# State sum by accumulating transfers, y times gate on GpSimd, d and du repeated inside SBUF, conv norm's moments on ScalarE, with new order tables

## The chip, the cores and the metric

The kernel runs on one core of a Trainium2 chip. The metric is the device time of one execution in microseconds (us); the median of several executions is given. PE is TensorE (matrix products into PSUM), DVE VectorE, ACT ScalarE, POOL GpSimd, and SP SyncE, which only starts transfers. POOL reads and writes SBUF alone, not PSUM. Each engine takes its instructions strictly in order, so an instruction that waits holds up all that stands behind it on its engine.

## The reference, cut to what matters

The input x is (4, 64, 64, 96): four images of L = 4096 tokens with C = 96 channels. Layer 0 normalizes (group norm, then a layer norm over the channels, called c norm here), projects each token to value u, gate, delta d and three blocks A, B, C of 96 x 16 states, and runs a recurrence along the tokens:

```
proj = layernorm(groupnorm(x)) @ W_in + b_in
value, delta = proj[..., :C], proj[..., 2*C:3*C];  gate = sigmoid(proj[..., C:2*C])
h_new = d * (A_t * h) + d * (B_t * u)          # per channel and state, S = 16
y = gate * sum over states of (C_t * h_new)
x = x + y @ W_out + b_out
```

Layer 1 adds a linear attention (no softmax, six heads, so that it comes down to one matrix per image made from the Gram matrix of the normalized tokens) and a feed-forward block in fp8 with fp16 rounding, each behind a layer norm (a norm and f norm).

## The kernel before, in words

An image is cut into NCH = 8 chunks of TC = 512 tokens; the N = 32 chunks of all images, called groups g here, run one after the other, since the recurrence goes along them. A group is NT = 12 tiles: four blocks sh of four states each, times three blocks cg of 32 channels. A tile is 128 partitions (4 states x 32 channels) by 512 tokens. There are K = 384 tiles, and the main loop makes one step per tile (the loop over s at the end of the kernel). In step s it issues, in this order: the B projection of tile s+3 (three matmuls into the one bank B) and its copy to SBUF with bias on ACT (`b_copy`, L888), the A projection of tile s+1, the C projection of tile s, ACT's copy of the last state, on POOL the multiply of B by du for tile s+2 (`b_mul`, L891) and, where the tile is one of the list ON_POOL, the multiply of C by h of tile s-1 (`c_mul_pool`, L940), on DVE the scan of tile s (L907), the A multiply by d of tile s+1 (`a_mul`, L900) and, for tiles not on ON_POOL, the C multiply (`c_mul`, L931, reads PSUM). For a tile on ON_POOL, ACT first copies C from PSUM to SBUF (`c_copy`, L937). Then everything that the table AT puts at this step is issued (`call(step)`).

AT is an order written out by hand: it names for each piece of work a step relative to the first step s0 of its group. Negative steps prepare a group ahead, steps of 12 and more finish it beside the next group's tiles, and the FFN of a group runs 96 steps later (beside the next image), at its own offsets. Work that would fall behind step K goes to a planner (`Plan`), which orders the end by costs, ranks and a random search; another such plan orders the start.

What the change touches, with its lines:

- d and du: `d_out` (ACT, L786) and `du_out` (DVE, L790) leave d and d*u of a group in `dd`, 96 partitions by 2 x 512. The tiles need them repeated for each of the four states of a partition block: `write` (L824) sends `dd` to DRAM, and `read` (L831) reads it back four times, once per block of 32 partitions, into `rep` (two buffers). SP starts both.
- the state sum: the products of C and h lie in one buffer of 3 x 512 per block sh (`slot`, L925): block 0 in the ring "cha" of two, blocks 1, 2, 3 in the ring "chb" of three. `gather` (L946) adds each of blocks 1, 2, 3 into block 0's buffer by an accumulating transfer started on POOL, at steps 7, 11 and 14. `state_sum` (L955, step 18) sums the four states on the partitions and turns them to channels with three matmuls against the matrix `fold` into PSUM; an fp32 matmul shows as two instructions. `gated` (DVE, L993, step 18) multiplies that by the gate.
- the norms: `LayerNorm.stats` makes mean and variance on DVE (four BATCH_NORM_STATS2, L433, and four BATCH_NORM_AGGREGATE, L435). `Roots.root` on POOL adds eps (L406), raises to the power -1/2 (L409), negates the mean (L412) and multiplies it (L413). `apply` on ACT (L450) scales and shifts, with two pointer operands.
- x tiles wait in XBUFS = 15 buffers from `load_x` to `total`, where the output is formed.

## Time and profile before

Three runs of the kernel took 1170.11 us in the median (1169.56 to 1172.9). The profiled execution:

| what | value |
|---|---|
| time of the profiled execution | 1169.27 us |
| its span, first to last instruction | 1167.5 us |
| mean granted clock of TensorE | 0.992 |
| first scan of the first group; first scan of the last group; end of the last scan | 35.1; 1073.1; 1104.0 us |
| groups of image 0 and 1 (35.1 to 303.0) | 32 to 36 us each |
| groups 17 to 25 (600.2 to 871.4) | 33.4 to 34.7 us each |
| the end (1104.0 to 1167.5): busy DVE, ACT, POOL | 48.5, 44.2, 24.8 us of 63.5 |
| accumulating gathers (768 KB), start to landing, median | 6.6 us |
| read of rep (384 KB each of four); write of dd | 7.3; 3.2 us |
| DVE's waits, all: on the out projection (L1003) | 17.2 us in 29 times |
| B's weight loads waiting for ACT | 22.5 us in 33 times |

The page's groups give a line of the code, engine, operation, tiles written and read, shapes and count, then busy time and mean duration, then the idle time ahead of them. In the timeline each row has start, duration, engine, line and operation; rows marked x4 are four instructions merged. A busy share says how full an engine is, but instructions of one engine overlap at their ends, and TensorE's ends are modelled, so the distance between starts is the better price of an instruction on a full engine.

### The profile page before, as it was taken

To read this page: it belongs to the slowest core of one execution; us is meant where nothing else is said; L and a number is where in the kernel's file an instruction comes from. 1 tells how busy PE (TensorE), PEld (TensorE's weight loads), DVE (VectorE), ACT (ScalarE), POOL (GpSimd) and SP (SyncE) were. 2 spreads that over 40 slices of the span, in tenths; PEclk is the share of its full clock that TensorE was granted. 3 is DMA by queue.
4 is the path that set the end of the run, shared out by engine and by line. 5 is a ranking of instruction groups with operands and counts; after the bars stand their busy time and mean duration, and the time that the engine had idled before them with its cause. 6 is when DMAs were issued, how large, how long until landed. Compare 5 with 4: busy or idle time off the path is not lost. (4 is left out here: it accounts for less than half of the span.)

```text
span 1167.5 us, 19144 instructions
## 1 busy us (share of the span) xinstructions
PE 1129.6 (97%) x5868; PEld 865.4 (74%) x5868; DVE 1116.8 (96%) x2110; ACT 811.3 (69%) x1818; POOL 1008.9 (86%) x1166
## 2 busy tenths in 40 slices
PE   6999999999999999999999999999999999999984
PEld 5777776777777777777877777777777777777662
DVE  6999999999999999999999999999999999999986
ACT  4666656555556777777777777787777777776477
POOL 5798888888889899899999999999999999988643
PEclk7999999999999999999999999999999999999999
DMA  7577777787776777687777778667776876777321
GB/s 183 137 167 146 165 158 160 157 178 164 166 162 151 161 166 175 148 185 162 159 163 167 165 165 189 149 152 159 167 172 149 183 160 157 150 161 166 78 82 55
DMA packets 104289, 182.13 MB, mean 156 GB/s; under 512 B 42637, under 2 KB 50769, under 8 KB 104186
## 3 DMA queue, kind: packets, MB, share of 16 engines
q1 hardware_dynamic: 90060, 106.96, 38.9%
q0 software_dynamic: 13536, 73.93, 31.8%
q8 instruction: 46, 0.75, 0.3%
q14 instruction: 57, 0.47, 0.1%
q10 hardware_dynamic: 590, 0.02, 0.0%
HBM read 69.12 MB, written 24.77 MB: 80 GB/s over the span
## 5 line engine op out<-in xcount | busy, mean ns | idle before, releaser
L891 POOL TENSOR_TENSOR bu<-bu,rep 128x512 f32<-128x512 f32 x384 | 511.3, 1342 | 51.1 <-ACT state L917 39.7
L907 DVE TENSOR_TENSOR_SCAN h<-Aps,state,bu 128x512 f32<-128x512 f32 x336 | 426.1, 1268 | 0.3 <-issue 0.2
L888 ACT ACTIVATE bu<-Bps,b_bac 128x512 f32<-128x512 f32 x384 | 262.8, 684 | 198.7 <-PE Bps L283 190.8
L900 DVE SCALAR_TENSOR_TENSOR Aps<-Aps,b_bac,rep 128x512 f32<-128x512 f32 x384 | 281.8, 734 | 3.6 <-PE Aps L283 3.1
L283 PE MATMUL Bps<-xs,w 128*128 128x512 f32 x768 | 266.9, 429 | 3.4 <-ACT bu L888 3.1
L283 PE MATMUL Aps<-xs,w 128*128 128x512 f32 x768 | 241.7, 395 | 1.2 <-DVE h L907 1.0
L940 POOL TENSOR_TENSOR ch<-ch,h 128x512 f32<-128x512 f32 x126 | 168.1, 1334 | 9.7 <-ACT ch L937 5.1
L283 PEld LDWEIGHTS Aps<-xs,w 128*128 128x128 f32 x768 | 143.6, 188 | 37.2 <-DVE h L907 2.9
L283 PEld LDWEIGHTS Bps<-xs,w 128*128 128x128 f32 x768 | 126.5, 190 | 45.5 <-ACT gx_ps L632 12.6
L283 PE MATMUL Aps<-xl,w 128*128 128x512 f32 x384 | 151.8, 395 | 0.0
L283 PE MATMUL Bps<-xl,w 128*128 128x512 f32 x384 | 151.4, 394 | 0.0
L283 PE MATMUL Cps<-xs,w 128*128 128x512 f32 x384 | 120.6, 395 | 0.0
L283 PE MATMUL Dps<-xs,w 128*128 128x512 f32 x384 | 120.6, 395 | 0.0
L931 DVE SCALAR_TENSOR_TENSOR ch<-Dps,b_bac,h 128x512 f32<-128x512 f32 x160 | 118.6, 741 | 0.4
L946 POOL DMA_DIRECT2D ch<-ch x94 | 88.7, 944 | 2.3 <-DMA ch<-ch 1.7
L283 PEld LDWEIGHTS Aps<-xl,w 128*128 128x128 f32 x384 | 72.0, 188 | 17.8
L283 PEld LDWEIGHTS Bps<-xl,w 128*128 128x128 f32 x384 | 72.2, 188 | 17.5
L283 PEld LDWEIGHTS Cps<-xs,w 128*128 128x128 f32 x384 | 72.0, 188 | 17.6
L283 PEld LDWEIGHTS Dps<-xs,w 128*128 128x128 f32 x384 | 72.0, 188 | 17.6
L937 ACT ACTIVATE ch<-Cps,b_bac 128x512 f32<-128x512 f32 x94 | 64.5, 686 | 24.3 <-PE Cps L283 24.3
L283 PE MATMUL Cps<-xl,w 128*128 128x512 f32 x192 | 75.7, 395 | 0.0
L283 PE MATMUL Dps<-xl,w 128*128 128x512 f32 x192 | 75.6, 394 | 0.0
(203 smaller groups left out, 2013.7 us busy)
## 6 DMA issues: line engine op xcount, KB each, us to landing
ch<-ch POOLq DMA_DIRECT2D x94, 768.0 KB, 6.6
rep<-ddd SPq DMA_DIRECT2D x124, 384.0 KB, 7.3
ddd<-dd SPq DMA_DIRECT2D x31, 384.0 KB, 3.2
xl<-lo SPq DMA_DIRECT2D x62, 128.0 KB, 2.4
x<-in_x_dram SPq DMA_DIRECT2D x32, 192.0 KB, 3.0
xatd<-xat SPq DMA_DIRECT2D x32, 192.0 KB, 3.8
xal<-xatd SPq DMA_DIRECT2D x32, 192.0 KB, 3.4
out_dram<-o SPq DMA_DIRECT2D x32, 192.0 KB, 3.4
```

What stands on the lines that cost most here:

```text
L283: nc.tensor.matmul(ps, lhsT=wt[:, n], rhs=mv, start=(n == 0), stop=(n == 2))
L888: nc.scalar.activation(self.bu, self.b_ps, AF.Identity, bias=self.bias(0))
L891: nc.gpsimd.tensor_tensor(self.bu, self.bu, rep[self.b, self.i][:, 1, self.cg], ALU.mult)
L900: nc.vector.scalar_tensor_tensor(self.a_ps, self.a_ps, self.bias(1), rep[self.b, self.i][:, 0, self.cg], ALU.add, ALU.mult,)
L907: nc.vector.tensor_tensor_scan(self.h, self.a_ps, self.bu, 0.0 if self.i == 0 else state[self.sh, self.cg], ALU.mult, ALU.add,)
L931: nc.vector.scalar_tensor_tensor(self.slot(), self.c_ps, self.bias(2), self.h, ALU.add, ALU.mult)
L937: nc.scalar.activation(self.ch, self.c_ps, AF.Identity, bias=self.bias(2))
L940: nc.gpsimd.tensor_tensor(self.ch, self.ch, self.h, ALU.mult)
L946: nc.gpsimd.dma_start(chs[g, 0], chs.pop((g, sh)), accum_op=ALU.add)
```

## The change

- **State sum.** The buffer into which the blocks are gathered is that of block 1 (of block 0 in the very first group), it lies in ring "cha", and the others lie in "chb". After three gathers, two more accumulating transfers on POOL halve it, 128 to 64 to 32 partitions (`halve64`, `halve32`), and `collect` (three transfers on SP) puts the result on 96 partitions in a new buffer y. The three matmuls go, but for the last group, which keeps them in the plan of the end.
- **Gated** runs on POOL from y in place of DVE from PSUM; the last group stays on DVE.
- **d, du.** `spread` copies from `dd` to `rep` inside SBUF: four calls of three transfers each, and `rep` has its dimensions in another order. The write to DRAM and the reads go.
- **c norm.** In groups 2 to 31 its moments come from ACT: four activations with accumulation for the sums, one for the mean with its sign, four squares with accumulation, and one for variance plus eps. The two groups of the start stay on DVE.
- **All norms.** POOL keeps the power and the product; eps and the negated mean come from two small ACT instructions (`shifts_scalar`) in the a and f norms of the main part, from DVE in the start and the end.
- **Tables.** AT has new steps, image 0 has a table AT0 of its own, ON_POOL has three tiles per group in place of four (1, 2, 9; in image 0 0, 5, 9, of which the first group has only 9), and the end has other ranks, pairs, costs, seed and choices of engine.

The diff, cut to its core:

```diff
 AT = {
-    "load_x": -39, "centre": -25, "scale": -24, "stats": -22, "rstd": -22, "apply": -21,
-    "transpose": -14, "affine": -13, "upper": -13, "low": -12, "proj_d": -9, "d_out": -9,
-    "proj_u": -9, "du_out": -9, "write": -9, "read": -6, "proj_gate": -3, "gate_out": -1,
-    "gather1": 7, "gather2": 11, "gather3": 14,
-    "state_sum": 18, "gated": 18, "project_out": 19, "residual": 19, "stats_a": 20,
-    "rstd_a": 21, "apply_a": 22, "transpose_a": 33, "keep": 34, "spill": 39, "gram": 24,
-    "gram_out": 24, "gram_add": 26,
-    "fetch": 21, "attention": 26, "residual_f": 26, "stats_f": 26, "rstd_f": 27, "apply_f": 29,
-    "transpose_f": 30, "quant_in": 31, "hidden0": 37, "relu0": 37, "hidden1": 31, "relu1": 33,
-    "hidden2": 38, "relu2": 38, "project_f": 40, "round_out": 40, "bias_out": 40, "total": 46,
-    "store": 51,
-    "sums": -31, "sums_out": -30,
+    "load_x": -35, "centre": -28, "scale": -27, "stats": -26, "squares": -24, "rstd": -22,
+    "apply": -20, "transpose": -14, "affine": -13, "upper": -13, "low": -12, "proj_d": -9,
+    "d_out": -9, "proj_u": -8, "du_out": -8, "spread0": -7, "spread1": -5, "spread2": -5,
+    "spread3": -5, "proj_gate": 0, "gate_out": 3, "gather1": 7, "gather2": 10, "gather3": 13,
+    "halve64": 15, "halve32": 18, "collect": 21, "state_sum": 22, "gated": 24,
+    "project_out": 25, "residual": 25, "stats_a": 26, "shift_a": 26, "rstd_a": 26,
+    "apply_a": 29, "transpose_a": 35, "keep": 35, "spill": 36, "gram": 30, "gram_out": 30,
+    "gram_add": 30, "fetch": 23, "attention": 26, "residual_f": 26, "stats_f": 27,
+    "shift_f": 28, "rstd_f": 28, "apply_f": 29, "transpose_f": 30, "quant_in": 30,
+    "hidden0": 37, "relu0": 37, "hidden1": 31, "relu1": 32, "hidden2": 38, "relu2": 38,
+    "project_f": 39, "round_out": 39, "bias_out": 41, "total": 48, "store": 54, "sums": -30,
+    "sums_out": -30,
 }
 MV_BUFS = {1: 4, 2: 2}
-END_RANKS = (-2, 0, 1)
-END_PAIR = (0, 1, 1, 2, 2, 3, 3, 4)
-APPLY_DVE = (0, 2, 4, 6, 7)
-QUANT_POOL = (1, 4)
-BIAS_DVE = (0, 1, 2, 3, 4, 5, 6, 7)
-TOTAL_DVE = (1, 3, 5, 7)
-ON_POOL = (0, 2, 7, 8)
+END_RANKS = (-5, 1, -1)
+END_PAIR = (0, 1, 2, 3, 4, 5, 6, 6)
+APPLY_DVE = (1, 2, 6)
+QUANT_POOL = (0, 1, 2, 3, 5, 7)
+BIAS_DVE = (0, 3, 4, 5, 6, 7)
+TOTAL_DVE = (0, 3, 4, 5, 6)
+ON_POOL = (1, 2, 9)
+AT0 = {
+    "load_x": -35, "centre": -30, "scale": -27, "stats": -24, "rstd": -21, "apply": -17,
+    "transpose": -14, "affine": -13, "squares": -23, "upper": -13, "low": -13, "proj_d": -10,
+    "d_out": -10, "proj_u": -9, "du_out": -9, "spread0": -8, "spread1": -7, "spread2": -6,
+    "spread3": -6, "proj_gate": 0, "gate_out": 3, "gather1": 7, "gather2": 11, "gather3": 14,
+    "halve64": 16, "halve32": 19, "collect": 20, "state_sum": 22, "gated": 23,
+    "project_out": 24, "residual": 24, "stats_a": 26, "rstd_a": 26, "apply_a": 28,
+    "transpose_a": 29, "keep": 33, "spill": 36, "gram": 30, "gram_out": 30, "gram_add": 31,
+    "shift_a": 26,
+}
+ON_POOL0 = (0, 5, 9)
 XBUFS = 15
-END_TRIES = 1500
+END_TRIES = 250
+END_SEED = 43
...
-            n = len(self.of)
-            for k, ln in enumerate(self.of):
-                if k and ln.eps == self.of[k - 1].eps:
-                    continue
-                m = k + 1
-                while m < n and self.of[m].eps == ln.eps:
-                    m += 1
-                nc.gpsimd.tensor_tensor(
-                    self.r[:, k:m], self.mv[:, k:m, :, 1], eps_t[ln.eps][:, 0 : m - k], ALU.add
-                )
-            nc.gpsimd.tensor_tensor(self.r, self.r, mhalf[:, 0:n], ALU.pow)
-            if not shift:
-                return
-            nc.gpsimd.tensor_tensor(self.nmr, self.mv[:, :, :, 0], minus[:, 0:n], ALU.mult)
-            nc.gpsimd.tensor_tensor(self.nmr, self.nmr, self.r, ALU.mult)
+            nc.gpsimd.tensor_tensor(self.r, self.r, mhalf[:, 0 : len(self.of)], ALU.pow)
+            if shift:
+                nc.gpsimd.tensor_tensor(self.nmr, self.nmr, self.r, ALU.mult)
...
+            if not late:
+                self.shifts(shift)
+        def shifts(self, shift=True):
+            nc.vector.tensor_scalar(self.r, self.mv[:, :, 1], self.eps, None, ALU.add)
+            if shift:
+                nc.vector.tensor_scalar(self.nmr, self.mv[:, :, 0], -1.0, None, ALU.mult)
+        def shifts_scalar(self):
+            nc.scalar.activation(self.r, self.mv[:, :, 1], AF.Identity, bias=eps_t[self.eps])
+            nc.scalar.activation(self.nmr, self.mv[:, :, 0], AF.Copy, scale=-1.0)
+        def sums(self, src):
+            self.group = Roots()
+            self.group.of.append(self)
+            self.group.tiles()
+            t = small.tile([P, J], F32, tag="lns", name=f"lns_{self.nm}", bufs=2)
+            for j in range(J):
+                nc.scalar.activation(
+                    src[:, j, :], src[:, j, :], AF.Identity, accum_out=t[:, j : j + 1]
+                )
+            nc.scalar.activation(self.nmr, t, AF.Copy, scale=-1.0 / C)
+        def squares(self, src):
+            t = small.tile([P, J], F32, tag="lnq", name=f"lnq_{self.nm}", bufs=2)
+            for j in range(J):
+                nc.scalar.activation(
+                    junk, src[:, j, :], AF.Square, bias=self.nmr[:, j : j + 1],
+                    accum_out=t[:, j : j + 1],
+                )
+            nc.scalar.activation(self.r, t, AF.Identity, scale=1.0 / C, bias=eps_t[self.eps])
...
-        def write(self):
-            self.dr = dram.tile([2, C, TC], F32, tag="dd", name=f"ddd_{self.nm}", bufs=3)
-            nc.sync.dma_start(self.dr.rearrange("k p n -> p k n"), self.dd)
-        def read(self):
-            src = self.dr.rearrange("k (g c) n -> c (k g) n", c=32)
-            t = rep[self.b, self.i].rearrange("p k g n -> p (k g) n")
-            for q in range(4):
-                nc.sync.dma_start(t[q * 32 : (q + 1) * 32], src)
+        def spread(self, q):
+            t, dd = rep[self.b, self.i], self.dd
+            for cg in range(NCG):
+                nc.sync.dma_start(
+                    t[q * 32 : (q + 1) * 32, cg], dd[cg * 32 : (cg + 1) * 32]
+                )
...
-                ("centre", f.centre, nc.gpsimd), ("scale", f.scale, nc.gpsimd), ("stats", f.stats),
-                ("rstd", f.ln.rstd), ("apply", f.apply), ("transpose", f.transpose),
+                ("centre", f.centre, nc.gpsimd), ("scale", f.scale, nc.gpsimd), ("stats", f.sums),
+                ("squares", f.squares), ("rstd", f.ln.rstd), ("apply", f.apply), ("transpose", f.transpose),
                 ("affine", f.affine), ("upper", f.upper), ("low", f.low), ("proj_d", f.proj, 2),
                 ("d_out", f.d_out), ("proj_u", f.proj, 0), ("du_out", f.du_out),
-                ("write", f.write), ("read", f.read),
+                *((f"spread{q}", f.spread, q) for q in range(4)),
...
+    def base(g):
+        return 1 if g else 0
...
-            self.on_pool = self.r in ON_POOL and self.k >= START
+            self.on_pool = self.r in (ON_POOL if self.b else ON_POOL0) and START <= self.k < K - 1
...
                 chs[self.g, self.sh] = sb(
-                    "chb" if self.sh else "cha", [P, NCG, TC], F32, f"ch_{self.nm}"
+                    "cha" if self.sh == base(self.g) else "chb", [P, NCG, TC], F32, f"ch_{self.nm}"
...
-    def gather(g, sh):
-        nc.gpsimd.dma_start(chs[g, 0], chs.pop((g, sh)), accum_op=ALU.add)
+    def gather(g, n):
+        sh = [sh for sh in range(NSH) if sh != base(g)][n - 1]
+        nc.gpsimd.dma_start(chs[g, base(g)], chs.pop((g, sh)), accum_op=ALU.add)
+    def halve(g, n):
+        t = chs[g, base(g)]
+        nc.gpsimd.dma_start(t[0:n], t[n : 2 * n], accum_op=ALU.add)
+    y_sb = {}
+    def collect(g):
+        t, y = chs.pop((g, base(g))), sb("y", [C, TC], F32, f"y_{g}")
+        for cg in range(NCG):
+            nc.sync.dma_start(y[cg * 32 : (cg + 1) * 32], t[0:32, cg])
+        y_sb[g] = y
...
-        t = chs.pop((g, last or 0))
+        t = chs.pop((g, base(g) if last is None else last))
...
         def gated():
-            nc.vector.tensor_tensor(yg[0:C, :], y_ps.pop(g), gate.pop((b, i)), ALU.mult)
+            engine, y = (nc.gpsimd, y_sb.pop(g)) if g in y_sb else (nc.vector, y_ps.pop(g))
+            engine.tensor_tensor(yg[0:C, :], y, gate.pop((b, i)), ALU.mult)
...
+        def stats():
+            ln.stats(t, late=not phase["end"])
...
-            (("state_sum", state_sum, g), ("gated", gated)),
+            (("gated", gated),) if g < N - 1 else (("state_sum", state_sum, g), ("gated", gated)),
             (("project_out", project_out), ("residual", residual)),
-            (("stats_a", ln.stats, t),),
+            (("stats_a", stats), ("shift_a", ln.shifts_scalar)),
             (("rstd_a", ln.rstd),),
...
-            (("stats_f", ln.stats, t),),
+            (("stats_f", stats), ("shift_f", ln.shifts_scalar)),
```

In the end, the two shifts are made on DVE with the moments (`late` is false there), and the costs of the planner's jobs are set to the new instructions.

## The prediction, made before the changed kernel had run

> **What bounds the kernel now.** I read the page first (shares of the engines, costliest groups), then the tables by stage, then the timeline of one group of twelve tiles, engine by engine, then the table of waits. The first view is part 1 of the page.
>
> ```profile
> PE 1129.6 (97%) x5868; PEld 865.4 (74%) x5868; DVE 1116.8 (96%) x2110; ACT 811.3 (69%) x1818; POOL 1008.9 (86%) x1166
> ```
>
> Two engines at once look full, and a third nearly so. The stage table, cut at the first scans of groups 17, 18, 19 and 20, says the same of a steady stretch (columns: us; busy PE, PEld, DVE, ACT, POOL; clock; DMA share; GB/s).
>
> ```profile
> 600.19:634.88 34.69, 34.69 (x187) 26.89 (x187) 33.71 (x66) 26.57 (x62) 31.50 (x37) 1.00 0.74 164
> 634.88:668.80 33.92, 33.92 (x179) 26.17 (x179) 32.98 (x62) 26.55 (x61) 31.16 (x36) 1.00 0.74 162
> 668.80:702.72 33.92, 33.92 (x179) 26.17 (x178) 32.98 (x62) 26.56 (x61) 31.51 (x37) 1.00 0.77 173
> ```
>
> A group takes 33.92 us. DVE is idle for 0.94 of it, POOL for 2.4 to 2.8, ACT for 7.4; the clock is full. The 31 gaps between first scans take 1038 us of the span of 1167.5 (first scan at 35.1, last group's at 1073.1), so a microsecond per group is worth 31.
>
> Is DVE really without slack? Timeline of DVE in group 17 (start, duration, line, op):
>
> ```profile
> 600.19 1.27 DVE L907 TENSOR_TENSOR_SCAN h<-Aps,state,bu 128x512 f32<-128x512 f32 x1
> 601.38 0.73 DVE L900 SCALAR_TENSOR_TENSOR Aps<-Aps,b_bac,rep 128x512 f32<-128x512 f32 x1
> ...
> 604.45 0.74 DVE L931 SCALAR_TENSOR_TENSOR ch<-Dps,b_bac,h 128x512 f32<-128x512 f32 x1
> 605.11 1.27 DVE L907 TENSOR_TENSOR_SCAN h<-Aps,state,bu 128x512 f32<-128x512 f32 x1
> ...
> 606.94 0.72 DVE L433 BATCH_NORM_STATS2 st_c<-z 128x6 f32<-128x96 f32 x4
> 607.59 0.36 DVE L435 BATCH_NORM_AGGREGATE mv_c<-st_c 128x2 f32<-128x6 f32 x4
> 607.87 0.56 DVE L1164 TENSOR_TENSOR x<-a_ps,x 128x384 f32<-128x384 f32 x1
> ...
> 620.56 0.69 DVE L993 TENSOR_TENSOR yg<-y_ps,gate 96x512 f32<-96x512 f32 x1
> 621.17 0.24 DVE L1116 COPY rmat<-r_ps 97x96 f32<-97x96 f32 x1
> ```
>
> Each instruction starts some 0.09 us before its predecessor ends, so its price is the distance between starts, not its duration: scan 1.19, c multiply (L931) 0.66, the conv norm's moments 0.93 (606.94 to 607.87), gated 0.61 (620.56 to 621.17). In the waits of DVE the largest is the out projection, L1003, 17.2 us in 29 times; the scan waits 0.4 us for POOL in the whole run. DVE bounds the main part. PE is close behind, but "100% busy" is modelled; its timeline shows the price of the state sum:
>
> ```profile
> 619.12 0.40 PE L1174 MATMUL xq_ps<-ident,xn 128*128 128x128 fp8e5 x4
> 619.45 1.06 PE L955 MATMUL y_ps<-ch,fold 128*32 128x512 f32 x6
> 620.43 0.41 PE L1101 MATMUL r_ps<-kvff,w_qt 97*97 97x96 f32 x2
> ```
>
> 0.98 us from 619.45 to 620.43, once per group, with no gap on either side.
>
> **The change, part by part, per group of 12 tiles.**
>
> PE: the state sum goes for 31 groups (the last keeps it): 31 x 0.98 = 30.4 us.
>
> DVE: gated goes from 31 groups, 31 x 0.61 = 18.9; the conv norm's moments from the 30 fronts made in the main part, 30 x 0.93 = 27.9. Added: POOL multiplied 126 tiles by h (row L940); by the new lists it is 94 (three per group, one in group 0), so 32 more on DVE at 0.66, 21.1. The shifts of the attention and FFN norms go to ACT, not DVE. Net 18.9 + 27.9 - 21.1 = 25.7 us less. DVE loses less than PE, so DVE stays the bound of the two, at 32.98 - 0.61 - 0.93 + 0.66 = 32.1 per group.
>
> POOL: 32 x 1.25 = 40.0 less (an L940 slot in the timeline: 603.88 to 605.13). Each norm loses its add and its negation: 608.04 to 608.31 and 609.33 to 609.60, 0.27 each, 0.54 in three norms, 1.6 per group. Gated comes: 96x512 isn't in the trace on POOL; 128x384 takes 0.92 (L1236), 128x512 1.25, and its row length is that of the second: 1.25. Two more DMA starts per group: 0.66 (633.46 to 634.12) to 0.96, the mean duration; smaller transfers have no row, so 0 to 0.96, and I take 0.75. Per group -1.05 - 1.6 + 1.25 + 1.5 = +0.1: POOL stays at about 31.5.
>
> The Trainium skill's GPSIMD Engine Reference (4.1, Engine selection) speaks against moving gated: elementwise work belongs on VectorE, GpSimd being about twice as slow for two inputs. The two rows above agree on the factor (1.25 against 0.61), and counted as engine time the move loses 31 x 0.64 = 20 us; but POOL is idle for 2.4 us per group and DVE for 0.94, so I count what it takes off DVE.
>
> ACT: one c copy of 0.59 (617.91 to 618.50 for its like, L888) less. Eight activations over 128x96 with accumulation come: the z apply costs 0.36 each (1.54 for four), and reading an accumulator 0.22 (619.16 to 619.38), so 8 x 0.58 = 4.6; at the low end the reads hide, 2.9. Two results of 128x4 and four shifts at 0.08 (L917, 618.50 to 618.58) to 0.2: 0.5 to 1.2. Together +2.8 to +5.2 per group; I take 4.5, for the accumulator row is for the same instruction. ACT goes from 26.6 to about 31 of 33. Square and sigmoid already share one table load.
>
> The Trainium skill's ScalarE: Activation LUTs (What ACT_TABLE_LOAD costs) prices an activation without pointer operands at 186 ns + 0.833 ns per element, 93 ns more per pointer, with 93 ns of overlap: 0.17 and 0.27 at 96 elements. By an estimate from it ACT would gain 3.5 us in place of 4.5, which no row here shows.
>
> Transfers: the d, du round trip loses its write (384 KB, 3.2 us to landing) and reads SBUF in 12 pieces of 128 KB instead of four of 384 KB. The halvings and collect add 384 + 192 + 192 KB. DMA engines are at 0.74 to 0.77; gathers of 768 KB land in 6.6 us. So +0.4 MB in some 6 MB per group, hidden. SP issues some 23 transfers at about 0.45 us (four reads in 1.76) per group, 10 us of 33. Without the write rep is there some 3 us earlier. What could bite is in POOL's queue: the accumulating transfers go into the same buffer, so each start waits for the one before to land, and b and c multiplies stand behind it. From gather 3 (step 13) to halve64 (15) POOL has two b multiplies, two c multiplies (tiles 1, 2), two norm roots of 1.2 and the 0.96 of the start: 8.4 us against 6.6. Gather 1 to 2: about 7.9; 2 to 3: 6.9. In the first image 13 to 15 becomes 14 to 16 with about 4.7: up to 1.9 of wait, where POOL idles anyway. Taken as 0; ends 0 and 4 us per group.
>
> The later gated (24 for 18) delays only the tail; x tiles live 35 + 96 + 48 steps, within 15 buffers of 12 steps.
>
> The end: 63.5 us (1103.97 to 1167.5), ACT 44 busy, and the chain there is mainly ACT. Quantizing moves from ACT to POOL for four chunks (1.54 each, L1211) and two applies move to ACT (1.45): 3.2 off. Group 30's tail moves into it (gated, residual, moments, and an apply of 1.5 on ACT). I take -1, ends -6 and +5. The start is left at 0.
>
> **Sum.** The profiled execution took 1169.27 (span 1167.5 and 1.8 around it); the median of the runs is 0.8 higher. 1169.3 - 25.7 - 1 = 1142.6. Against it: DVE, PE, POOL and ACT will all be at 94 to 98%, coupled by one B bank and short rings. PE now waits for ACT before B in 33 places, 22.5 us in all (12.6 behind L632, 9.9 behind L888, longest 1.8); two bursts of 2.3 us on ACT per group make more of them. I add 4 us (0 to 20). 1146.6, on the median's footing 1147. Better bound: the new tables also halve DVE's idle 0.94 per group: 31 x 0.47 = 15 off, 1132.
>
> **Rivals.**
> 1. ACT holds the B bank. For: the row L632 above does it now with 1.3 us bursts. Against: ACT waits 190.8 us for B already, so it has room. One wait of 0.5 per group, none absorbed: 1147 - 4 + 15 = 1158.
> 2. POOL's queue held by landings: slower than before. Place: gathers 2, 3 and halve64. At a mean landing of 8.5 us the waits are 0.6 + 1.6 + 0.1 = 2.3, at 9.5 they are 1.6 + 2.6 + 1.1 = 5.3. POOL's 31.5 + 0.4 of small gaps leaves 2.0 to the old 33.92: it decides from about 8.4, and at 9.0 (3.8 of wait) a group takes 35.7, +1.8 on 24 groups: 1169 + 43 - 1 = 1211. For: gathers beside the rep reads land in 8 to 11.8 now. Against: the pieces leave right after du_out, ahead of gather 1, and the median is 6.6.
> 3. The freed PE and DVE time isn't on the path, because a group's order of waits sets its length: 1168, no change. Against: DVE's gap-free starts.
>
> **Chances.** Forecast (1139 to 1153) 0.52; tables close idle as well (1128 to 1139) 0.19; rival 1 (1153 to 1164) 0.17; rival 3 0.04; rival 2 0.08. Two executions differ by up to 0.3%, so within that is no change. Range 1131 to 1163: it leaves out about 0.05 below and 0.13 above. Faster 0.88, same 0.04, slower 0.08.
>
> **What would show it.** Right: L955 six instructions in all, a group of about 33.0 us in the stage table with DVE at 32.1 and ACT near 31; POOL's waits for DMA under 1 us per group. Wrong: DMA as releaser of POOL's starts above 2 us per group (rival 2), B's weight loads waiting for ACT by 0.5 per group more (rival 1), DVE's busy time unchanged (32 multiplies dearer than 0.66), or an end longer than 68 us.

## The result, and the profile after

The changed kernel took 1227.45 us in the median of four runs (1221.65 to 1231.4), the kernel before 1171.4 beside it (1169.56 to 1172.9): a ratio of 1.0475, 95% interval 1.0425 to 1.0526. It is slower, and 80 us above the forecast of 1147. The profiled execution took 1229.83 us with a span of 1228.1.

Cut at the same scans, the span grew by 60.6 us. The 31 gaps between first scans went from 1038.0 to 1087.1 (+49.1), the last group from 30.9 to 35.6, the end behind the last scan from 63.6 to 69.5, the start by 0.8. The eight groups of image 0, which have the table AT0 (35.1 to 297.7 us before), hardly changed (262.7 before, 263.4 after). The loss sits in images 1 to 3.

Part 1 and the clock row of part 2 of the page of the changed kernel:

```profile
PE 1142.9 (93%) x5677; PEld 891.1 (73%) x5677; DVE 1108.0 (90%) x1884; ACT 900.6 (73%) x2436; POOL 1034.9 (84%) x1054
...
PEclk8999998999999999999999899999999999998878
```

DVE was at 96% and PE at 97%; now no engine is full, so the kernel waits. The granted clock was full between 600 and 1103 us before; now it is 0.98 and 0.95 in the first two stages below and 0.75 in the end. The table by stage is cut at first scans and at the end of the last scan, with the same columns as before:

```profile
615.90:902.50 286.60, 270.94 (x1378) 213.03 (x1377) 261.99 (x434) 232.45 (x633) 255.96 (x262) 0.98 0.79 167
902.50:1158.60 256.10, 235.23 (x1154) 183.20 (x1152) 225.29 (x372) 180.93 (x472) 217.51 (x215) 0.95 0.72 152
1158.60:1228.10 69.50, 56.09 (x371) 39.80 (x371) 49.70 (x208) 42.38 (x88) 34.54 (x38) 0.75 0.25 66
```

The first row is eight groups of images 2 and 3, 35.8 us each. DVE stands for 24.6 of 286.6 us, where it stood for 0.94 in 33.92 before. The waits tell for whom (us in total, times, longest):

```profile
DVE x L1043 <- PE o_ps L1038: 57.1, 31, 3.5
PEld o_ps L1038 <- POOL yg L1033: 50.8, 24, 4.9
PE o_ps L1038 <- POOL yg L1033: 43.1, 21, 4.5
...
POOL bu L917 <- DMA rep<-dd: 32.1, 10, 4.8
```

Read from below: POOL's multiply of B by du (L917) waits for the repeated d and du; y times gate (L1033), now on POOL too, comes late; PE stands in front of the out projection (L1038); DVE stands in front of the residual behind it (L1043). The timeline of one such place, POOL, PE and DVE:

```profile
865.98 1.29 POOL L917 TENSOR_TENSOR bu<-bu,rep 128x512 f32<-128x512 f32 x1 [2.28 <-ACT bu L914]
...
872.45 1.52 POOL L1033 TENSOR_TENSOR yg<-y,gate 96x512 f32<-96x512 f32 x1
```

```profile
874.02 0.97 PEld L1038 LDWEIGHTS o_ps<-w_o,yg 97*128 97x128 f32 x8 [2.40 <-POOL yg L1033]
```

```profile
875.20 0.56 DVE L1043 TENSOR_TENSOR x<-o_ps,x 128x384 f32<-128x384 f32 x1 [2.46 <-PE o_ps L1038]
```

POOL's 2.28 us reappear as 2.40 on PE and 2.46 on DVE. The first line names ACT's copy of B as what ended the wait, but the copy that ended just then (865.72) is for a later tile. The one that this multiply needs (ACT, L914, started at 860.75, 0.67 us long) had ended 4.55 us before POOL started, over groups 9 to 30 1.4 to 5.9 us before. What POOL waited for is the pieces of `rep`: here the piece that SP started at 857.25 landed at 865.85, and POOL began at 865.98. The table of waits names them for the groups in which they came last. SP's queue ahead of this place shows when they left:

```profile
850.98 1.82 SPq L852 DMA_DIRECT2D rep<-dd  x3
852.84 0.59 SPq L1283 DMA_DIRECT2D out_dram<-o  x1
853.47 7.24 SPq L852 DMA_DIRECT2D rep<-dd  x9
```

`du_out` ended at 850.95, 17.8 us into its group (18.1 in the mean of groups 9 to 30, 12.3 before). Twelve pieces keep SP busy until 860.71. From the end of `du_out` to SP's last start of a piece it is 9.7 us in the mean, 4.8 for the write and four reads before. POOL's idle time ahead of the first B multiply of a group was 0 before and is 2.64 us (mean of groups 9 to 30).

The lateness also seems to feed itself. `du_out` moved by one step, but it ends 18.1 us into its group in place of 12.3, while the same step in the kernel before gives 15.1 (experiment 16). Ahead of `du_out` in DVE's order lies the residual, where DVE stands for the late out projection. This is read from the order and these numbers; no run tests it by itself.

### The profile page after: what moved, and what is told of

It is laid out like the page before. It is cut to its first block, busy times and chain, and to the rows that moved or that the text cites. A ratio compares the mean times of both kernels' runs of the same rounds, so it can differ in the third digit from the quotient of the medians.

```text
span 1228.1 us, 20028 instructions
## 1 busy us (share of the span) xinstructions
PE 1142.9 (93%) x5677; PEld 891.1 (73%) x5677; DVE 1108.0 (90%) x1884; ACT 900.6 (73%) x2436; POOL 1034.9 (84%) x1054
## 5 line engine op out<-in xcount | busy, mean ns | idle before, releaser
L917 POOL TENSOR_TENSOR bu<-bu,rep 128x512 f32<-128x512 f32 x384 | 567.7, 1524 | 81.3 <-DMA rep<-dd 32.1
L914 ACT ACTIVATE bu<-Bps,b_bac 128x512 f32<-128x512 f32 x384 | 262.3, 683 | 159.0 <-PE Bps L289 155.1
L289 PE MATMUL Aps<-xs,w 128*128 128x512 f32 x768 | 248.9, 406 | 9.0 <-DVE h L933 8.7
L289 PEld LDWEIGHTS Bps<-xs,w 128*128 128x128 f32 x768 | 129.9, 193 | 34.8 <-ACT bu L914 19.0
L289 PE MATMUL Aps<-xl,w 128*128 128x512 f32 x384 | 155.1, 404 | 0.0
L966 POOL TENSOR_TENSOR ch<-ch,h 128x512 f32<-128x512 f32 x94 | 135.6, 1442 | 3.6 <-ACT ch L963 3.4
L289 PE MATMUL Cps<-xs,w 128*128 128x512 f32 x384 | 124.2, 405 | 0.0
L957 DVE SCALAR_TENSOR_TENSOR ch<-Cps,b_bac,h 128x512 f32<-128x512 f32 x161 | 119.6, 743 | 0.0
L973 POOL DMA_DIRECT2D ch<-ch x94 | 93.9, 999 | 13.0 <-DMA ch<-ch 3.2
L957 DVE SCALAR_TENSOR_TENSOR ch<-Dps,b_bac,h 128x512 f32<-128x512 f32 x129 | 95.9, 743 | 0.2
L289 PEld LDWEIGHTS Dps<-xs,w 128*128 128x128 f32 x384 | 73.5, 191 | 18.1
L1038 PE MATMUL o_ps<-w_o,yg 97*128 97x96 f32 x256 | 39.9, 304 | 43.9 <-POOL yg L1033 43.1
```

Source lines behind the costliest of these rows:

```text
L289: nc.tensor.matmul(ps, lhsT=wt[:, n], rhs=mv, start=(n == 0), stop=(n == 2))
L914: nc.scalar.activation(self.bu, self.b_ps, AF.Identity, bias=self.bias(0))
L917: nc.gpsimd.tensor_tensor(self.bu, self.bu, rep[self.b, self.i][:, self.cg, 1], ALU.mult)
L957: nc.vector.scalar_tensor_tensor(self.slot(), self.c_ps, self.bias(2), self.h, ALU.add, ALU.mult)
L966: nc.gpsimd.tensor_tensor(self.ch, self.ch, self.h, ALU.mult)
L973: nc.gpsimd.dma_start(chs[g, base(g)], chs.pop((g, sh)), accum_op=ALU.add)
```

## The experiments

Ratios are against runs of the kernel before on the same chip. "Main part" is the 31 gaps between first scans, "stands" are stretches over 0.5 us in it without a matmul or weight load, "half clock" is the whole time at a granted clock of 0.5. The changed kernel has 1087.1 us of main part, 25 stands with 50.9 us, and 111.5 us of half clock; the kernel before has 1038.0, 4 with 3.7, and 20.9. Diffs of the tables are cut to the entries that change. The first four experiments were made on the theory that twelve pieces in place of a write and four reads make `rep` late. The rivals: POOL has too much work, or the clock halves for a reason of its own.

**1. rep_by_dram**: d and du through DRAM again, in the new layout.

```diff
-            for cg in range(NCG):
-                nc.sync.dma_start(t[q * 32 : (q + 1) * 32, cg], dd[cg * 32 : (cg + 1) * 32])
+            self.dr = dram.tile([C, 2, TC], F32, tag="dd", name=f"ddd_{self.nm}", bufs=3)
+            nc.sync.dma_start(self.dr, self.dd)
...
+            for q in range(4):
+                nc.sync.dma_start(t[q * 32 : (q + 1) * 32], src)
```

> The changed kernel with d and du repeated by way of DRAM again (one write of 384 KB, four reads of 384 KB), in the new layout of rep; all else as changed. Theory 1 (late rep: the 12 small transfers leave SP over 11 us, the first b multiply of the next group waits for them and holds POOL's queue, gated comes late, PE stands before the out projection and its clock is halved afterwards): POOL's idle time before the b multiply falls from 81 us to about 50, PE's idle stretches over 0.5 us in the main part from 51 us to under 15, half-clock time from 112 to under 40 us, time 1150 to 1165. Theory 2 (POOL has too much work with gated and two more DMA starts per group, wherever rep comes from): nothing moves, 1210 to 1235. Theory 3 (the clock is halved for a reason of its own): half-clock time stays at about 110 us, 1195 or more.

Measured 1267.45 us, 1.0812 (1.0755 to 1.0868). SP's last start came 5.3 us behind `du_out` instead of 9.7, yet POOL waited as long (2.54 us) and the stands grew to 74.4 us. Of the three theories only the third, whose range is open, has room for this time and for the half clock of 121 us. The number of pieces alone isn't the cause; against this round trip (write at step -7, reads at -5) the pieces are a gain of 40 us.

**2. gated_23**: y times gate one step earlier.

```diff
-    "halve64": 15, "halve32": 18, "collect": 21, "state_sum": 22, "gated": 24,
+    "halve64": 15, "halve32": 18, "collect": 21, "state_sum": 22, "gated": 23,
```

> The changed kernel with gated of images 1 to 3 at step 23 in place of 24; POOL's work is the same, only its order. Theory 1: the b multiply still waits for rep (about 80 us of idle), but y times gate is done some 3 us earlier, so PE no longer stands before the out projection: PE's idle stretches under 15 us in the main part, half-clock under 45 us, time 1150 to 1170. Theory 2: the work that POOL can't do in time is now the b multiply, the scan waits for it (over 20 us in all, 2.5 now), time 1205 to 1230. Theory 3: 1195 or more.

Measured 1202.49, 1.026 (1.0234 to 1.0286): 25 us less from one step in POOL's order. Stands 26.3 us, half clock 63.3, waits for y times gate 18.6 us. The place in POOL's queue matters, but theory 1's range is missed by 32 us, and half of the stands remain.

**3. gated_dve**: y times gate on DVE, from y in SBUF.

```diff
-            engine, y = (nc.gpsimd, y_sb.pop(g)) if g in y_sb else (nc.vector, y_ps.pop(g))
+            engine, y = (nc.vector, y_sb.pop(g)) if g in y_sb else (nc.vector, y_ps.pop(g))
```

> The changed kernel with y times gate on DVE, from the same y in SBUF; the state sum stays with the transfers. Theory 1: PE doesn't stand for yg, since DVE is not held by rep; DVE has 31 times 0.61 us more: 1155 to 1175, with POOL's wait for rep still there. Theory 2: POOL has 39 us less to do, and its idle time grows by about as much; 1150 to 1165. Theory 3: 1200 or more.

Measured 1260.17, 1.0765 (1.0712 to 1.0819), though POOL is relieved. The groups of its page show the reason (count, busy us, mean ns):

```profile
L1033 DVE TENSOR_TENSOR yg<-y,gate 96x512 f32<-96x512 f32 x31 | 96.0, 3095 | 1.5 <-DMA y<-ch 1.5
```

The same product took 681 ns with y in PSUM (21.8 us for 32 in the kernel before). With both inputs in SBUF it takes 3095 in the mean and 676 at its shortest, 74 us more in all. So this run says nothing on POOL's queue; it shows another price.

**4. project_26**: out projection and residual at 26, the a norm's moments at 27.

```diff
-    "project_out": 25, "residual": 25, "stats_a": 26, "shift_a": 26, "rstd_a": 26,
+    "project_out": 26, "residual": 26, "stats_a": 27, "shift_a": 27, "rstd_a": 27,
```

> The changed kernel with out projection, residual and the attention norm's moments and root of images 1 to 3 one step later (26, 27). Theory 1: a step of 2.5 to 3 us covers most of yg's delay: PE idle stretches under 20 us, half-clock under 50 us, 1155 to 1175. Theory 2: POOL is still late by the same work, part of the wait goes: 1190 to 1220. Theory 3: 1200 or more.

Measured 1210.71, 1.0351 (1.0302 to 1.04): stands 30.8 us, half clock 45.3. Asking for y times gate later also helps, by 17 us. That lies in theory 2's range, not in theory 1's; experiment 6 decides between them.

**5. fold_pe**: the state sum on PE and y times gate on DVE from PSUM (not for the last two groups).

```diff
-            (("gated", gated),) if g < N - 1 else (("state_sum", state_sum, g), ("gated", gated)),
+            (("gated", gated),) if g == N - 2 else (("state_sum", state_sum, g), ("gated", gated)),
...
-            if g < N - 1:
+            if g == N - 2:
                 at(s0 + table(b)["halve64"], halve, g, 64)
```

> State sum back on PE (three matmuls into the M bank, at step 22) and y times gate back on DVE from PSUM (step 24), for all groups but the last two; no halvings and no collect there; all else as in the changed kernel. Theory A (y times gate stands last in POOL's full queue, PE stands in front of the out projection for it, and its clock is halved after each such stand): POOL is out of that chain, so the stands of over 0.5 us (25, 50.9 us in the main part) fall below 20 us, half clock from 111.5 below 50 us; PE gets 29 x 0.98 and DVE 29 x 0.61 of work back; time 1160 to 1190. Theory B (the group got longer by its transfers and the order tables, PE's stands are a result): 1205 to 1230, the stands move to another wait. Theory C (the clock halves for a reason of its own): half clock stays above 90 us.

Measured 1194.96, 1.0201 (1.0155 to 1.0248). Stands fell to 17.6 us, half clock to 57.0, the main part to 1060.0, although PE and DVE got some 28 and 18 us of work back by the forecast's prices (DVE's busy time there grew by 15.4). POOL's wait at the first B multiply fell only to 1.07, but nothing on PE hangs on it. The time is 5 us above theory A's range; the end took 73.1 us here.

**6. du_early**: the steps of image 0 for d and du in all images.

```diff
-    "low": -12, "proj_d": -9, "d_out": -9, "proj_u": -8, "du_out": -8,
-    "spread0": -7, "spread1": -5, "spread2": -5, "spread3": -5,
+    "low": -13, "proj_d": -10, "d_out": -10, "proj_u": -9, "du_out": -9,
+    "spread0": -8, "spread1": -7, "spread2": -6, "spread3": -6,
```

> Images 1 to 3 get the steps of the first image for d and du: low at -13, the d projection at -10, the u projection and du at -9, spreads at -8, -7, -6, -6. All else as in the changed kernel. Theory A1 (du is made a step late, its pieces land late, POOL waits 2.6 us per group for them at the first b multiply and reaches y times gate that much later): POOL's wait there falls below 0.5 us, PE's stands from 50.9 below 25 us, time 1185 to 1205. Theory A2 (POOL's queue is late by its own work and the pieces' landing is only where it shows): the wait moves to another place of POOL's queue, time 1218 to 1235.

Measured 1182.69, 1.0088 (1.0061 to 1.0116): 45 us less from a handful of numbers. The line of the B multiplies, first in the page of the changed kernel, then in that of this one:

```profile
L917 POOL TENSOR_TENSOR bu<-bu,rep 128x512 f32<-128x512 f32 x384 | 567.7, 1524 | 81.3 <-DMA rep<-dd 32.1
```

```profile
L917 POOL TENSOR_TENSOR bu<-bu,rep 128x512 f32<-128x512 f32 x384 | 578.2, 1560 | 15.8 <-ACT bu L914 5.6
```

Its idle time falls from 81.3 to 15.8 us and the transfer is gone as releaser, although SP still needs 9.3 us from `du_out` to the last piece. POOL does the same work (theory A2 falls; the time is 2 us below A1's range). PE's wait for y times gate goes from 50.8 us in 24 times to 4.7 in 8, half clock to 60.4. The waits name what is left:

```profile
DVE x L1205 <- PE a_ps L1200: 32.6, 26, 1.5
...
PEld a_ps L1200 <- ACT dd L813: 16.7, 20, 0.8
...
PEld o_ps L1038 <- POOL yg L1033: 4.7, 8, 1.7
```

**7. moments_dve**: the c norm's moments back on DVE.

```diff
-                ("centre", f.centre, nc.gpsimd), ("scale", f.scale, nc.gpsimd), ("stats", f.sums),
-                ("squares", f.squares), ("rstd", f.ln.rstd), ("apply", f.apply), ("transpose", f.transpose),
+                ("centre", f.centre, nc.gpsimd), ("scale", f.scale, nc.gpsimd), ("stats", f.stats),
+                ("rstd", f.ln.rstd), ("apply", f.apply), ("transpose", f.transpose),
```

> The c norm's moments back on DVE (four moments and four aggregates at step -26, and the two shifts behind them), nothing of them on ACT; all else as in the changed kernel. DVE gets 30 x 0.93 = 27.9 us plus its shifts back, ACT loses about 30 x 3.2. If DVE's work still sets the group as forecast: 1240 to 1260. If POOL's late y times gate and PE's stands set it (theory A), DVE has idle time to take it in: 1220 to 1235. If the bursts on ACT are what makes the rest late (theory D): below 1215.

Measured 1243.19, 1.0612 (1.0584 to 1.0641), 16 us more. DVE's work grew by 48.8 us, more than the 27.9 of the moments: adding eps to 128x4 values, which comes with them here and stood on POOL before, cost 0.68 us each, up to 5.4. So the moments' price isn't isolated by this run.

**8. du_gated_project**: experiments 6, 2 and 4 together.

```diff
-    "low": -12, "proj_d": -9, "d_out": -9, "proj_u": -8, "du_out": -8,
-    "spread0": -7, "spread1": -5, "spread2": -5, "spread3": -5, "gated": 24,
-    "project_out": 25, "residual": 25, "stats_a": 26, "shift_a": 26, "rstd_a": 26,
+    "low": -13, "proj_d": -10, "d_out": -10, "proj_u": -9, "du_out": -9,
+    "spread0": -8, "spread1": -7, "spread2": -6, "spread3": -6, "gated": 23,
+    "project_out": 26, "residual": 26, "stats_a": 27, "shift_a": 27, "rstd_a": 27,
```

> Three moves of the tables together: d and du early (as in du_early), y times gate at step 23, and out projection 26, a norm's moments 27. Theory A with additive parts: 1227 less 25 (y times gate a step earlier) less 17 (out projection a step later) less up to 20 (early du): 1165 to 1190, stands below 10 us, half clock below 30 us in the main part. If the parts take away the same stands twice: 1190 to 1205. If late pieces are not it and the steps only push the wait on: about 1200 to 1215.

Measured 1205.16, 1.029 (1.0261 to 1.0319): 22 us worse than du_early alone. The time lies in the third range, but late pieces are gone (POOL's wait ahead of the first B multiply is 0.01 us): the two other moves helped only while y times gate was late. Now out projection and attention share a step, and DVE waits 52.3 us for the former (57.1 in the changed kernel, 10.9 in du_early).

**9. du_only**: du_early without its spreads.

```diff
-    "low": -12, "proj_d": -9, "d_out": -9, "proj_u": -8, "du_out": -8,
+    "low": -13, "proj_d": -10, "d_out": -10, "proj_u": -9, "du_out": -9,
```

> Of du_early only the first half: low -13, d projection -10, u projection and du -9; the spreads stay at -7, -5, -5, -5 as in the changed kernel. du_early took 1182.7 us, the changed kernel 1227.5. If the late du decides (its end 12.9 us into the group in du_early, 18 in the changed kernel) and the pieces follow it anyway: 1180 to 1195, POOL's wait ahead of the first b multiply under 0.5 us. If the step at which SP gets the nine later pieces decides (step -5, two to three steps before the first b multiply): the wait stays above 1.5 us and the time is 1210 to 1230.

Measured 1189.39, 1.0139 (1.011 to 1.0168), POOL's wait 0.17 us. The step of du decides; the steps at which SP gets the pieces are worth some 7 us more.

**10. du_residual_27**: du_early with the attention's residual a step later.

```diff
-    "attention": 26, "residual_f": 26,
+    "attention": 26, "residual_f": 27,
```

> du_early with the residual of the attention one step later (27 for 26), ahead of its moments in the same step; nothing else. In du_early DVE stands 29.2 us in the main part for the attention's matmuls, 26 times up to 1.5 us, since the residual is issued in the step of the attention. If these stands are DVE's own loss: 1182.7 less 15 to 29, so 1154 to 1168, faster than the kernel before. If PE is what bounds there and the residual only shows it: 1178 to 1186, and the idle time turns up at another instruction of DVE.

Measured 1189.27, 1.0171 (1.0113 to 1.0228). The idle time moved: in the profiled execution, 13 us above this median, DVE waits 40.9 us for the A projection instead (4.9 in du_early). So the order of DVE was not the loss; PE was behind.

**11. du_fold_pe**: du_early and fold_pe together.

```diff
-    "d_out": -9, "proj_u": -8, "du_out": -8,
+    "d_out": -10, "proj_u": -9, "du_out": -9,
... (the other entries as in experiment 6, the halvings as in 5)
-            (("gated", gated),) if g < N - 1 else (("state_sum", state_sum, g), ("gated", gated)),
+            (("gated", gated),) if g == N - 2 else (("state_sum", state_sum, g), ("gated", gated)),
```

> du_early with the state sum back on PE and y times gate on DVE for all groups but the last two (as in fold_pe): the price of the moved state sum when d and du come in time. PE gets 29 x 0.98 = 28 us and DVE 29 x 0.61 = 18 us of work back, POOL loses 29 x 1.25 and two starts. If DVE's work sets the group as forecast: 1182.7 plus about 18, 1195 to 1210. If the move only gave DVE and PE time that they then spend waiting: 1178 to 1188. If POOL's late y times gate still costs (9.9 us of waits for the out projection in du_early): below 1175.

Measured 1221.56, 1.0423 (1.0388 to 1.0457), above all three ranges: with du early moving the state sum back to PE costs 39 us, 31.6 of them in the main part: DVE's work is 18.1 us greater and its idle time 13.4. With late du the same move back saved 32 us (5). Nor is the 39 the price of the sum alone: steady groups take 34.9 us here and 33.6 in experiment 5, since here PE also waits for ACT's d at the attention.

**12. awake**: eight small matmuls ahead of each out projection, their result overwritten.

```diff
+            for j in range(0 if phase["end"] else 2 * J):
+                nc.tensor.matmul(
+                    ps[:, j % J, :], lhsT=ident, rhs=ident[:, 0:C], start=True, stop=True
+                )
```

> The changed kernel with eight small matmuls (128x128 by 128x96, about 1 us in all, result overwritten) on PE ahead of each out projection of the main part, so that PE is busy during the first part of its wait for y times gate. The stands of PE (2 to 4.5 us) get about 1 us shorter. If the half clock follows stands of over some 2 us and costs time of its own: half clock from 111.5 to 40 to 80 us, time 1195 to 1222. If the half clock comes whatever PE does, or costs nothing because PE has to wait anyway: 1222 to 1240, some of it added by the matmuls in the groups in which PE did not wait.

Measured 1229.51, 1.0492 (1.0467 to 1.0517). Stands fell to 23.4 us and half clock to 54.3, and the time stayed: DVE's wait for the out projection went from 51.8 to 70.0 us in the main part. With POOL late as before (2.3 us), less half clock bought nothing that the extra matmuls didn't take. The half clock accompanies the stands; a small price of its own can't be excluded by this run.

**13. du_step9**: du a step earlier, d left where it is.

```diff
-    "d_out": -9, "proj_u": -8, "du_out": -8, "spread0": -7, "spread1": -5, "spread2": -5, "spread3": -5,
+    "d_out": -9, "proj_u": -9, "du_out": -9, "spread0": -8, "spread1": -7, "spread2": -6, "spread3": -6,
```

> The changed kernel with du one step earlier only (u projection and du at -9 instead of -8, as in the kernel before) and the spreads at -8, -7, -6, -6; the d projection stays at -9, a step behind the attention. In du_early (d at -10, the attention's step) the attention's matmuls waited 16.7 us for ACT's copy of d, and DVE 29.2 us behind them. If that bank wait is the rest of the main part: these waits gone, main part 1047 less 20 to 30, time 1150 to 1168, faster than the kernel before. If du then comes too late again, since d and u follow in one step: POOL's wait for the pieces above 1 us per group, 1195 to 1215. If PE is full whatever the order: 1178 to 1188.

Measured 1177.44, 1.0049 (1.0029 to 1.0069): 50 us below the changed kernel, but 9 above the range that the attention's wait was to give. That wait is gone (32.6 to 2.1 us on DVE), but d and u now share a step, and DVE waits for ACT's copy of d:

```profile
DVE dd L817 <- ACT dd L813: 22.9, 23, 3.3
```

Two steady groups by stage:

```profile
979.00:1012.10 33.10, 32.97 (x170) 25.31 (x169) 32.17 (x55) 28.53 (x79) 32.58 (x35) 1.00 0.88 180
1012.10:1045.20 33.10, 32.97 (x170) 25.28 (x169) 32.17 (x55) 27.17 (x70) 30.83 (x32) 1.00 0.85 174
```

That is the forecast's steady group: DVE 32.17 of 33.10 us (32.1 foreseen), clock full. Over all 31 gaps a group takes 33.6 us.

**14. step9_moments_dve**: du_step9 with the moments on DVE (the diff of 7).

> du_step9 with the c norm's moments and shifts back on DVE. The forecast priced them at 27.9 us of DVE: if DVE sets the group there, du_step9 plus 20 to 30 us. If PE sets it: du_step9 plus 0 to 8. In the changed kernel with late du the same edit cost 16 us.

Measured 1315.65, 1.1184 (1.1135 to 1.1233), far outside all expectations. DVE and POOL in its timeline:

```profile
1020.50 2.80 POOL L917 TENSOR_TENSOR bu<-bu,rep 128x512 f32<-128x512 f32 x2
1020.80 0.37 DVE L429 BATCH_NORM_AGGREGATE mv_c<-st_c 128x2 f32<-128x6 f32 x4
1021.20 5.43 DVE L434 TENSOR_SCALAR rstd_c<-mv_c 128x4 f32<-128x4 f32 x1
1022.98 1.19 POOL L1280 TENSOR_TENSOR o<-x,yb 128x384 f32<-128x384 f32 x1
1023.85 1.53 POOL L1033 TENSOR_TENSOR yg<-y,gate 96x512 f32<-96x512 f32 x1
1025.07 1.52 POOL L917 TENSOR_TENSOR bu<-bu,rep 128x512 f32<-128x512 f32 x1
```

Four values per partition take DVE 5.43 us. It starts inside a run of POOL instructions without a gap, and ends at 1026.63, where that run ends (1026.59). Such additions cost 101.7 us here (30 of 3.39), though the edit cost 16 us at other steps in experiment 7. The same instruction took 0.17 us at its shortest, where POOL stood, 4.76 in the median and 6.45 at its longest. So this run doesn't tell whether DVE or PE sets the steady group.

**15. step9_end_before**: du_step9 with the end's constants of the kernel before.

```diff
-END_RANKS = (-5, 1, -1)
+END_RANKS = (-2, 0, 1)
...
```

> du_step9 with the constants of the end from the kernel before (ranks, pairs, which chunks are applied, quantized, biased and summed on which engine, 1500 tries). The end took 63.6 us before and 65 to 73 in the kernels of this study, with 3 to 37 us of it at half clock. If the new constants make the end longer: 2 to 6 us less than du_step9, end at 62 to 65. If the group before it and the clock do: within 2 us of du_step9. If the new constants are a gain, as forecast (1 us): 1 to 5 us more.

Measured 1176.37, 1.0027 (1.001 to 1.0045), within 2 us of du_step9; its end takes 67.9 us against 65.4. So the new constants don't lengthen the end.

**16. before_late**: the kernel before with du and its transfers a step later.

```diff
-    "proj_u": -9, "du_out": -9, "write": -9, "read": -6,
+    "proj_u": -8, "du_out": -8, "write": -8, "read": -5,
```

> The kernel before with u projection, du and the write one step later (-8 for -9) and the read at -5 for -6: the same lateness as in the changed kernel. There y times gate is on DVE and needs nothing of POOL. If lateness hurts only through y times gate behind POOL's multiplies: POOL waits 1 to 3 us per group for the pieces but PE doesn't stand for it, 1170 to 1185. If every kernel pays for a late rep, through the scan that needs POOL's product: 1195 to 1230.

Measured 1179.85, 1.0063 (1.0045 to 1.0081). PE has stands of 10.7 us, and POOL's wait for `rep` is this:

```profile
POOL bu L891 <- DMA rep<-ddd: 18.2, 9, 3.2
```

The move that costs 45 to 50 us in the changed kernel costs 7 here. But the lateness isn't the same, as the expectation had assumed: `du_out` ends 15.1 us into its group (18.1 in the changed kernel), SP's last start comes 4.5 us behind it (9.7), and POOL's idle time ahead of the first B multiply is 0.48 us per group (2.64), not 1 to 3. How much of the difference is y times gate on DVE, and how much the shorter wait, this run doesn't separate.

**17. early_gate_4 and 18. step9_gate_4**: the gate's projection and sigmoid behind the crowded steps, with du_early and with du_step9.

```diff
-    "proj_gate": 0, "gate_out": 3,
+    "proj_gate": 4, "gate_out": 5,
```

> du_early with the gate's projection at step 4 and its sigmoid at 5 (0 and 3 in the changed kernel): the M bank that the gate holds over steps 0 to 3 is free for the out projection, the hidden layers, d and the attention. If the held bank makes the attention wait for ACT's copy of d: PE's 16.7 us and DVE's 29.2 us of waits there gone, 1182.7 less 20 to 30, 1152 to 1163, faster than the kernel before. If the bank isn't it: within 4 us of 1182.7, the waits unchanged.

> du_step9 with the gate's projection at step 4 and its sigmoid at 5. ACT's sigmoid (0.6 us) no longer stands ahead of the copy of d, and the bank is free. If these make DVE wait for the copy of d (22.9 us): 1177.4 less 12 to 23, 1154 to 1165, faster than the kernel before. If not: within 4 us of 1177.4.

Measured 1179.09, 1.0082 (1.0049 to 1.0116), and 1194.74, 1.0179 (1.0158 to 1.02). The first is within 4 us of du_early, as foreseen for a bank that isn't the cause: the steady groups fall to 33.2 us and PE no longer waits for ACT's d at the attention, but DVE still stands 23.7 us there, and other groups take 41.2, 37.9 and 37.2 us. The second is 17 us worse, outside both its ranges. The held bank is a part of the loss at most, and no version here beats the kernel before; du_step9 and its variant 15 come closest.

## Why the prediction was wrong, by its own steps

The forecast missed by 80 us. Experiment 13 takes back 50 of them by moving du one step earlier, with its pieces behind it. The other 30 are there even with du in time: in its profiled execution the main part is 26 us longer than foreseen and the end 3.

- **The steady group: right once du is in time.** 33.0 us with DVE at 32.1 was foreseen, and 33.10 with 32.17 is there in experiment 13. That DVE sets it, as forecast, isn't shown: PE is busy for 32.97 us in the same rows, and giving DVE more work (11, 14) never cost what was foreseen. The prices of DVE's parts hold too: the further c multiplies cost 20.4 us (21.1 foreseen), the moments gave 27.9 (27.9) and gated 18.1 (18.9).
- **Transfers: the step that failed.** "Without the write rep is there some 3 us earlier" takes `du_out` as where it was. The table has it a step later, and the spreads at -7 and -5; I worked through the shortened path and not the moved start. It ends 5.8 us later in its group. The path isn't shorter either: SP's twelve issues were counted as load (10 of 33 us), not as delay. From the end of `du_out` it is 9.7 us to SP's last start and 4.2 (median) to landing, 13.9 together, where the way over DRAM took 4.8 and 7.3, or 12.1. So `rep` came some 8 us later into the group, not 3 earlier, and POOL waited 2.64 us per group for it, a term that the sum doesn't have.
- **"The later gated (24 for 18) delays only the tail": wrong.** It is what makes the lateness dear. PE issues in order, the out projection stands one step behind gated, and no slack was left between POOL's place for gated and PE's need. Experiments 2, 4 and 5 show it from three sides; 16 fits, though POOL's wait was shorter there.
- **Rival 2 (POOL held by landings, 1211) had the kind, not the place.** Gathers and halvings hardly waited (3.2 us at L973); the pieces of `rep` did. Its condition, over 2 us per group, names the sign that came: 2.64 ahead of the first B multiply, though the releaser's own line gives only 32.1 us, since the view puts a part down to ACT.
- **Rivals 1 and 3.** ACT holding the B bank did not come: B's weight loads wait 19.0 us for it in place of 22.5. Rival 3, that a group's order of waits sets its length, had a chance of 0.04. With du in time it is the nearest: DVE has 17 us less work in the main part, and the kernel is still not faster than before.
- **POOL +0.1 us per group: +0.3.** Its busy time in the main part went from 941.4 to 951.5 us. The sum's -1.05 for the c multiply doesn't follow from its own row (one of 1.25 less per group).
- **DVE 25.7 us less: 11.4 in the changed kernel, 17 with du in time.** Five small instructions, for the group norms (L661) and the biases (L379), take 8.7 us more: the longest, a cast of 128x3, took 4.98 us and ended 0.16 us after a run of POOL instructions did. The rest of the difference in the changed kernel is longer slots of scan and A multiply.
- **Coupling 4 us: too small.** In du_step9 DVE stands 45.9 us in the main part against 24.1 before, 22.9 of it for ACT's d. That is 17.8 above the foreseen (24.1 and 4), and DVE's work is 8.5 above it: together the main part's 1042.6 in place of 1016.3. That further moves of the table always exchanged one such wait for another is shown for 8 and 10, and in part for 17; what order would avoid all of them stays open.
- **ACT +4.5 us per group: 2.9.** Sums took 0.18 us and squares 0.28 each, their accumulator reads 0.12 and 0.19, where 0.36 and 0.22 were taken. The Trainium skill's ScalarE: Activation LUTs (What ACT_TABLE_LOAD costs), with 0.17 and 0.27, was nearer for the activations.
- **End -1: +5.9, the size and sign wrong.** At 69.5 us it is above the 68 that was named as a sign of being wrong. Over the twenty kernels the end takes 63.6 to 73.1 us, and goes with its time at half clock (correlation 0.82, a quarter of a us per us). That is a correlation; only the constants of the end were tried and excluded (15). The cause stays open.

## What to carry to other kernels

In an order written out by hand, a step moved by one place is an edit like any other: follow its product to the first instruction that needs it, through every queue on the way, before counting engine time. An instruction moved to another engine inherits all that this engine waits for, and the in-order engine behind it pays; so the same move of du by one step cost 7 us in the kernel before, with y times gate on DVE, and 45 to 50 with it on POOL (where POOL's own wait was longer too, 2.64 us per group against 0.48). And when the name in a wait had long been done, take the next candidate that landed at that moment.

## What the runs showed of the hardware

- **DVE is held by POOL in some forms.** The product of two SBUF operands took 3.1 us in the mean beside a busy POOL, 0.68 at its shortest and 0.68 with one operand in PSUM (3); an addition of 128x4 in SBUF took 0.17 to 6.45 us (14). Scans and multiplies with an operand in PSUM were not held so (means of 1271 and 740 ns in 3, 1268 and 741 before). The Trainium skill's SBUF — State Buffer (Who interferes with whom) says that both forms can contend with GpSimd for a port pair that the two engines share, and that whoever issues first holds it for its whole instruction while the other blocks (said there of the two-port modes). The row of 5.43 us in 14 agrees that DVE blocks, but the block went on over several POOL instructions in a row.
- **Half clock follows short stands.** In the main parts of all twenty kernels, a half-clock interval began within 7 us of 24 of 296 stands of 0.5 to 1.7 us, of 23 of 49 of 1.7 to 2 us, of 43 of 60 of 2 to 3 us, and of all 62 longer ones. The intervals last 3.4 us or multiples of it. The Trainium skill's TensorE: Matmul & The Clock Gate (Part 1: The HAM clock gate) has the same 3.4 us, but as the idle time that it takes; here 1.7 to 2 us, about half of that, was enough in 23 of 49 cases.
- **Many small transfers delay more than they load.** SP's issue of a 128 KB piece within SBUF took 0.6 us, some up to 2.2, so the last of twelve left 9.7 us after its data were there; even so the way over DRAM was 40 us slower as a whole (1).
